# An LSTM recurrence on one core: smaller rooms for filler sums at the start, fewer sums in empty steps, and the first half of the late cells handed over in two pieces of 32 columns

## The chip, the cores and the metric

The kernel runs on one core of one Trainium2 chip. The metric is the device time of one execution in microseconds (us); the kernel before takes 3074.94 us, the median of three runs (3074.21 to 3075.44). All data are fp32.

## The reference, cut to what matters

The reference is an LSTM over 512 steps with a residual. Batch is 32, the input width 512, the hidden width 512.

```
xW = einsum('ntd,dg->ntg', x, Wx) + b        # x: 32 x 512 x 512, Wx: 512 x 2048
c = zeros_like(h0)
for each step t:
    a = xW[:, t] + h @ Wh                    # Wh: 512 x 2048
    i, f, o = sigmoid(a[:, :512]), sigmoid(a[:, 512:1024]), sigmoid(a[:, 1024:1536])
    g = tanh(a[:, 1536:])
    c = f * c + i * g
    h = o * tanh(c)
    out[:, t] = x[:, t] + h
```

## The kernel before, in words

**Steps.** The main loop goes over the 512 steps, `k`. A step has two parts on TensorE (PE). First comes the recurrent product `h @ Wh` of this step into the `gates` banks: 64 matmul instructions, in `h_part` (L1018) up to step 471 and in `h_halves` (L1032) from step 472 on, the "half steps". Then come products for the `x @ Wx` of later steps (L693, in the last steps also L935). While PE does these, the cell of the step is worked out: ScalarE (ACT) makes sigmoids and tanh (L1055 to L1057), VectorE (DVE) makes `fc`, `ig` and `c` (L1058 to L1060), ACT the tanh of `c` (L1061), DVE the product with the output gate (L1062) and its transposition into `ht` (L1063). The next recurrent product needs `ht`. So each step has two chains side by side, PE's filling products and the cell, and the longer one sets when the next recurrent product begins.

**x @ Wx.** These products are made for whole blocks of 32 steps (a "run") by a fast bilinear scheme: sums of input blocks ("nodes", L624; four small sums `s` per product, L652 to L655), products with sums of weight blocks, and sums of the products (L753, L763, L893, and L909 for the late ones, on DVE). Two short schemes for pairs of rows come first, and the weight sums are made once by DVE in the first steps (L452) and kept in memory (`keep_a`, `keep_b`). The program counts in window numbers `v = k + 16`; the runs begin at `v = START = 39` and take 32 steps each. Below, "rest n" is the n-th step of such a run. In the numbers n of a run's products there are gaps: some steps begin no product.

**The filler on DVE.** All DVE work that is not bound to the cell goes through a list. `push(window, columns, fn, ready)` enters a sum with the window number by which it has to be done; `run_due(v, room)` takes from the list what is due, and also what is not yet due as long as the room (in columns, 160 more for each sum) is not used up. The main loop calls it with `HEAD_ROOM` (5000) in the first steps, `ROOM` (4300) later and `HALF_ROOM` (2000) in the half steps. `evacuate`, which empties the PSUM banks of finished products, calls it once more, ahead of `third_sum` (`pp<-acc,p`, L763), with `BETWEEN` (1300) or, when no product was begun two windows before, twice that. What `run_due` takes in a step stands on DVE ahead of that step's `fc` (L1058), because the engine works in the order of the program.

**Half steps.** `cell_halves` works on 64 of 128 columns at a time. `gates_of(m)` has ACT make the gate functions of half `m` (L1077 to L1079), `sums_of(m)` has DVE make `fc`, `ig` and `c` (L1083 to L1085), ACT makes the tanh (L1098 and L1111), and `end_of(m)` has DVE multiply (L1089) and transpose (L1093). `h_halves` begins with `ht` of the columns of half 0, `k` = 0 and 1 (blocks of 32 columns of `ht`), into both halves of the gates, then takes `k` = 2 and 3. So PE's next step begins when the first half is transposed, and the second half has until the middle of the recurrent product.

**Ends.** The last sums of the last run go out in the first half steps; beside and after them come six late products (`describe_late`, with `t_sums`, weight sums on DVE at L405 to L407 into `nodes` and reloaded weights `raw_again`) and direct products (L935).

Of the kernel before, what the change touches and what calls it, by code (L numbers as in the profile page):

```python
# [15 lines left out]
B = 32  # L16
# [29 lines left out]
PER = ROW * MO  # L46
# [10 lines left out]
FIRST_SUMS = 1200  # L57
BETWEEN = 1300
HEAD_ROOM = 5000
FILL_ROOM = 3000  # L60
HALF_ROOM = 2000
SPACING = 5

LATE_ORDER = (1, 0, 2, 3, (0, (0, 1)), (0, (2, 3)))
# [252 lines left out]
def kernel(  # L317
# [400 lines left out]
    def evacuate(v, room):  # L718
        taken = run_due(v - 0.5, FIRST_SUMS if room else 0)
        taken += finish_halves(v)  # L720
        job = jobs.get(v - 1)
        if job and job.w >= EARLY:
            copy_first(job)
        for job in (jobs.get(v - 1), jobs.get(v - 2)):
            if job and job.w5 == v - 1 and job.w >= EARLY:
                copy_fifth(job)
        taken += second_sum(v)
        if v - 3 in jobs:
            taken += run_due(v, min(room - taken, BETWEEN if v - 2 in jobs else 2 * BETWEEN))
        return taken + third_sum(v)  # L730

    def evacuate_at_first(v):
# [140 lines left out]
    def finish_product(job, sb, n):  # L873
        c = sb.scheme

        def finish(half):
            pp = job.pp[half].rearrange("p n c -> p (n c)")
            if n in c.copied:
                if half == 0:
                    slot(sb, n)  # L880
                nc.scalar.copy(sums[sb, n][:, half], pp)

            def source(v):
                return pp if v == n else sums[sb, v][:, half]

            taken = 0

            for v in c.by_ready[n]:
                _, a, b = c.c_ops[v - c.r]
                if v in c.at_half:  # L890
                    if half == 0:
                        slot(sb, v)
                    add(c, v)(sums[sb, v][:, half], source(a), source(b))  # L893
                    taken += 4 * P + FIXED
                    if half == 1:
                        for u in (a, b):
                            if u != n or n in c.copied:
                                used(sb, u)
            if half == 0:
                return taken  # L900
            for v in c.by_ready[n]:
                if v in c.at_half:
                    put_out(sb, v)
                    continue

                def go(v=v):
                    _, a, b = c.c_ops[v - c.r]
                    slot(sb, v)
                    add(c, v)(sums[sb, v], sums[sb, a], sums[sb, b])  # L909
                    used(sb, a)  # L910
                    used(sb, b)
                    put_out(sb, v)

                push(
                    sb.at + c.limit[v] - 0.5,
                    8 * P,
                    go,
                    lambda at, v=v: all((sb, u) in sums for u in c.c_ops[v - c.r][1:])
                    and (last_use(sb, v) or len(sb.pool) > (at < sb.at + c.limit[v] - 0.5)),
                )  # L920
            return taken

        return finish
# [143 lines left out]
    def cell_halves(t):  # L1067
        n, tt = divmod(t, ROW)
        s = work.tile([P, G, P], F32, name=f"s_{t}", tag="s")
        fc = work.tile([P, P], F32, name=f"fc_{t}", tag="fc")  # L1070
        c = work.tile([P, P], F32, name=f"c_{t}", tag="c", bufs=2)
        ht = work.tile([P, NJ, B], F32, name=f"ht_{t}", tag="ht", bufs=3) if t < T - 1 else None
        us = [slice(m * HP, (m + 1) * HP) for m in range(2)]

        def gates_of(m):
            g, u = bank_half(m), us[m]
            nc.scalar.activation(s[:, 0:2, u], g[:, 0:2], AF.Sigmoid)  # L1077
            nc.scalar.activation(s[:, 2, u], g[:, 2], AF.Tanh)
            nc.scalar.activation(s[:, 3, u], g[:, 3], AF.Sigmoid)  # L1079

        def sums_of(m):
            u = us[m]
            nc.vector.tensor_mul(fc[:, u], s[:, 1, u], state["c"][:, u])  # L1083
            nc.vector.tensor_mul(ig[:, u], s[:, 0, u], s[:, 2, u])
            nc.vector.tensor_add(c[:, u], fc[:, u], ig[:, u])  # L1085

        def end_of(m):
            u = us[m]
            nc.vector.tensor_mul(fc[:, u], s[:, 3, u], ig[:, u])  # L1089
            if t == T - 1:  # L1090
                nc.vector.tensor_add(ig[:, u], fc[:, u], state["x"][:, u])
            else:
                nc.vector.transpose(ht[:, 2 * m : 2 * m + 2].rearrange("p q b -> p (q b)"), fc[:, u])  # L1093

        gates_of(0)
        seed_half(t + 1, 0)
        sums_of(0)
        nc.scalar.activation(ig[:, us[0]], c[:, us[0]], AF.Tanh)  # L1098
        if t == T - 1:
            gates_of(1)  # L1100
            sums_of(1)
            nc.scalar.activation(ig[:, us[1]], c[:, us[1]], AF.Tanh)
            end_of(0)
            end_of(1)
            nc.sync.dma_start(out=out[n][:, tt * P : (tt + 1) * P], in_=ig)
            return
        end_of(0)
        gates_of(1)
        seed_half(t + 1, 1)
        sums_of(1)  # L1110
        nc.scalar.activation(ig[:, us[1]], c[:, us[1]], AF.Tanh)  # L1111
        end_of(1)
        state["c"], state["ht"] = c, ht
        put_step(t)
# [78 lines left out]
    def describe_late(job, j):  # L1193
        def make(i):
            def begin():
                if not late_pairs:
                    assert len(node_free) == NODES
                    node_free.clear()
                    late_pairs.extend(node_pairs)
                tt_[i] = late_pairs.pop(0).rearrange("p m t e b -> p (m t e b)").rearrange("p (n c) -> p n c", c=C)  # L1200
                ops.extend(t_sums(i))
                ops.pop(0)()

            ops = []
            late_made[i] = []
            for m, columns in enumerate((2 * C, C, C)):

                def go(m=m):
                    (begin if m == 0 else ops.pop(0))()
                    late_made[i].append(m)  # L1210

                push(
                    job.w - 2 + 0.75 * m,
                    columns,
                    go,
                    lambda v, m=m: v >= LAST + 4 and len(late_made[i]) == m,
                )

        if isinstance(j, tuple):
            describe_half(job, *j)  # L1220
            return
        for i in (j, NJ + j):
            if i not in RESIDENT:
                make(i)
        if job.w == LATE_AT[0]:

            def both():
                f = free.pop(0).rearrange("p k (g t b) -> p k g t b", g=4, t=4)
                for k in range(2):
                    head_sums[LATE_ROW, k], more = inner_sums(block(raw_block(LATE_ROW, k)), f[:, k])  # L1230
                    late_ops.extend(more)
                late_ops.pop(0)()

            for m in range(8):
                push(
                    job.w - 2 + m / 4,
                    P,
                    lambda m=m: both() if m == 0 else late_ops.pop(0)(),
                    lambda v, m=m: v >= job.w - 2 and (len(late_ops) == 8 - m or m == 0),
                )  # L1240
        job.factors = lambda s: [
            (left(block(raw_block(LATE_ROW, k)), s, head_sums[LATE_ROW, k]), raw_factor(NJ * k + j, s)) for k in range(2)
        ]
        job.finish = finish_late(job, LATE_ROW, j)
# [52 lines left out]
    with tc.manual_schedule():  # L1297
# [70 lines left out]
        for k in range(T):  # L1368
            if k % 2 == 0 and k + 2 < T:
                load_residual(k + 2)  # L1370
            (h_part if k < HALVES else h_halves)(k)
            v = k + OFF
            if v < START + 14:
                head(v)
            announce(v)
            for op in prepare(v):
                op()
            room = HEAD_ROOM if v < START - 4 else ROOM if k < HALVES - 1 else HALF_ROOM
            run_due(v, room - evacuate(v, room))
            products(v)  # L1380
            tail_products(v)
            if k + 3 < LATE_END:
                load_xw(k + 3)
            fetch(v)
            if k == T - 2:
                x_last()
            if k + 4 < LATE_END:
                fill_bias(k + 4)
            (cell if k < HALVES else cell_halves)(k)
            seed_first(k + 2)  # L1390
            seed_last(k + 1)
# [52 lines left out]
```

## Time and profile before

| | before |
|---|---|
| median of 3 runs | 3074.94 us |
| profiled execution, its own time | 3074.57 us |
| its span | 3072.8 us |
| granted TensorE clock in it | 1.000 |
| DVE, ACT, POOL busy | 75%, 65%, 27% |
| DMA | 716.21 MB, 233 GB/s mean |

The span is the time between the first and the last recorded instruction of the profiled execution; its own time is 1.77 us longer. Busy time is given per engine, and the granted clock is the one at which TensorE was allowed to run. The chain of waits lists, in order of time, the piece of work that the end of the program depended on: start, length, engine, operation and line, number of instructions. In the groups of instructions the columns are line, engine, operation, tiles (out<-in), shapes and count, then total busy time and the mean ns of one, then the idle time just before them and what ended it. In the timeline a row has the start, the length, the engine, line and operation, and in brackets the idle time before it with what ended it. "issue" is time that the profile puts down to no wait.

### The profile page before, as it was taken

What the parts mean: (1) busy time and instruction counts of PE and PEld (TensorE: products, weight loads), DVE (VectorE), ACT (ScalarE), POOL (GpSimd) and SP (SyncE); (2) the same over time, 40 slices, a digit from 0 to 9 for tenths busy, and PEclk for the clock granted to TensorE, in tenths of its full rate; (3) what the DMA queues carried; (4) which work ended last, traced back from release to release, by engine and by line L of the source; (5) the groups of instructions that cost most, each with busy time, mean ns of one, the idle gap of its engine ahead of it and who ended that gap; (6) DMA issues with size and microseconds to landing.
All of it is one profiled execution on the core that took longest, in us unless ns stands there. A gap on an engine that the chain in (4) does not pass through costs nothing.

```text
span 3072.8 us, 133850 instructions
## 1 busy us (share of the span) xinstructions
PE 3064.4 (100%) x56568; PEld 2064.6 (67%) x56568; DVE 2314.5 (75%) x6545; ACT 2002.6 (65%) x5774; POOL 830.3 (27%) x1041
## 2 busy tenths in 40 slices
PE   9999999999999999999999999999999999999999
PEld 5566886666666666666666667866666666666666
DVE  7888777777777777777777777777777777777754
ACT  4666666666666666666666666666666666666664
POOL 0323222222222222222222222222222222222331
PEclk9999999999999999999999999999999999999999
DMA  9999887988889888898888988889788898888753
GB/s 326 294 271 268 233 247 213 255 231 236 246 210 259 224 244 238 218 263 216 254 231 212 267 214 248 232 223 260 216 254 232 223 255 222 250 232 219 196 120 71
DMA packets 345192, 716.21 MB, mean 233 GB/s; under 512 B 45712, under 2 KB 112016, under 8 KB 344080
## 3 DMA queue, kind: packets, MB, share of 16 engines
q1 hardware_dynamic: 268768, 564.74, 55.8%
q0 software_dynamic: 75392, 142.38, 27.6%
q8 instruction: 445, 7.29, 0.9%
q14 instruction: 155, 1.27, 0.1%
q10 hardware_dynamic: 432, 0.53, 0.1%
HBM read 521.48 MB, written 185.99 MB: 230 GB/s over the span
## 4 chain that ended last, share of the span: by engine, by line
PE 99%; DVE 1%; ACT 0%; DMA 0%; issue 0%; SPq 0%; DVEq 0%; ACTq 0%
PE gates L1018 53%; PE acc L693 18%; PE pp L693 18%; PE p L693 6%; PE gates L1032 4%; PE acc L935 0%; PE pp L935 0%; DMA raw_sb<-in_L_cond_Wx_dram 0%; DVE tt_sb L909 0%; PE gates L693 0%; DVE c L1085 0%; DVE fc L1089 0%; DVE fc L1083 0%; DVE ht L1093 0%; DVE nodes L405 0%
## 5 line engine op out<-in xcount | busy, mean ns | idle before, releaser
L1018 PE MATMUL gates<-wh_sb,ht 128*32 128x384 f32 (+1 forms) x30144 | 1739.2, 379 | 0.1
L1018 PEld LDWEIGHTS gates<-wh_sb,ht 128*32 128x32 f32 x30144 | 1083.8, 110 | 653.6 <-issue 554.9
L1121 POOL TENSOR_TENSOR oc<-xr,ht 128x128 f32<-128x128 f32 x509 | 384.6, 756 | 2101.8 <-DVE ht L1063 1916.6
L980 POOL DMA_DIRECT2D xw<-xw x508 | 447.1, 880 | 92.6 <-DVE s L652 62.5
L1055 ACT ACTIVATE s<-gates 128x256 f32<-128x256 f32 x472 | 182.0, 386 | 346.2 <-PE gates L1018 335.9
L693 PE MATMUL pp<-wb,nodes 128*32 128x256 f32 x4000 | 335.1, 379 | 0.0
L976 ACT COPY xw<-bias_sb 128x512 f32<-128x512 f32 x508 | 320.9, 632 | 0.0
L1058 DVE TENSOR_TENSOR fc<-s,c 128x128 f32<-128x128 f32 x471 | 136.6, 290 | 190.4 <-ACT s L1055 186.0
L761 ACT COPY pp<-pu 128x512 f32<-128x512 f32 x404 | 243.0, 602 | 47.5 <-DVE raw_sb L893 18.4
L1062 DVE TENSOR_TENSOR fc<-s,ig 128x128 f32<-128x128 f32 x472 | 137.8, 292 | 177.3 <-ACT ig L1061 177.3
L1057 ACT ACTIVATE s<-gates 128x128 f32<-128x128 f32 x472 | 131.2, 278 | 147.1 <-PE gates L1018 147.0
L693 PE MATMUL pp<-wb,s 128*32 128x256 f32 x2704 | 226.9, 379 | 0.0
L693 PE MATMUL acc<-wb,s 128*32 128x256 f32 x2704 | 226.9, 379 | 0.0
L693 PE MATMUL p<-wa,s 128*32 128x256 f32 x2704 | 226.7, 379 | 0.0
L763 DVE TENSOR_TENSOR pp<-acc,p 128x256 f32<-128x256 f32 x406 | 172.9, 426 | 71.4 <-ACT pp L762 69.0
L693 PE MATMUL acc<-wa,s 128*32 128x256 f32 x2704 | 226.4, 379 | 0.0
L1003 ACT COPY gates<-xw 128x384 f32<-128x384 f32 x472 | 223.2, 473 | 2.4 <-DMA xw<-xw 2.3
L762 ACT COPY pp<-acc 128x256 f32<-128x256 f32 x406 | 146.4, 361 | 108.0 <-DVE tt_sb L893 40.0
L1061 ACT ACTIVATE ig<-c 128x128 f32<-128x128 f32 x472 | 146.2, 310 | 101.0 <-DVE c L1060 60.8
L753 DVE TENSOR_TENSOR pu<-acc,p 128x256 f32<-128x256 f32 x404 | 167.4, 414 | 43.9 <-ACT p L772 35.4
L1063 DVE STREAM_TRANSPOSE ht<-fc 128x128 f32<-128x128 f32 x472 | 146.9, 311 | 50.3 <-DVE fc L1062 1.4
L772 ACT COPY p<-p 128x256 f32<-128x256 f32 x406 | 154.1, 379 | 37.1 <-PE p L693 34.9
(269 smaller groups left out, 4629.7 us busy)
## 6 DMA issues: line engine op xcount, KB each, us to landing
wb<-keep_b SPq DMA_DIRECT2D x338, 512.0 KB, 6.3
xw<-xw POOLq DMA_DIRECT2D x508, 256.0 KB, 5.8
wa<-keep_a SPq DMA_DIRECT2D x338, 384.0 KB, 5.3
xw<-tt_sb SPq DMA_DIRECT2D x404, 128.0 KB, 3.7
xw<-raw_sb SPq DMA_DIRECT2D x404, 128.0 KB, 3.9
xr<-in_x_dram SPq DMA_DIRECT2D x256, 128.0 KB, 5.5
out_dram<-oc SPq DMA_DIRECT2D x255, 128.0 KB, 4.5
row<-in_x_dram SPq DMA_DIRECT2D x63, 512.0 KB, 8.3
```

Source lines behind the costliest of these rows:

```text
L693: nc.tensor.matmul(dst[t * B : (t + 1) * B], a[:, t % a.shape[1]], w[t // a.shape[1]] if isinstance(w, list) else w, start=(s in (1, 5) or ...
L753: nc.vector.tensor_add(job.pu[:, 1], job.acc, job.p5)
L761: nc.scalar.copy(job.pp[0], job.pu)
L763: nc.vector.tensor_add(job.pp[1][:, 1], job.acc, job.p5)
L772: nc.scalar.copy(job.p5, p5[:, job.w if job.w < EARLY else 0])
L976: nc.scalar.copy(xw[t], bias_sb)
L980: nc.gpsimd.dma_start(out=xw[t], in_=stored[i][a], accum_op=mybir.AluOpType.add)
L1003: nc.scalar.copy(gates[t % 2][:, 0:IFG], xw[t][:, 0:IFG])
L1018: nc.tensor.matmul(g[j * B : (j + 1) * B, cols], state["ht"][:, k, :], wh_sb[:, k, j, cols], start=False, stop=True, skip_group_check=True,)
L1055: nc.scalar.activation(s[:, 0:2], g[:, 0:2], AF.Sigmoid)
L1063: nc.vector.transpose(ht.rearrange("p q b -> p (q b)"), h)
L1121: (nc.gpsimd if t < T - 3 else nc.vector).tensor_add(state["oc"][:, tt % 2], xr[t][:, tt % 2], ht)
```

## The change

Six small edits.

- In the main loop, up to `v = 38`, the room of a step is made smaller by 400 for every group of products that the step lacks (`FEWER`).
- In `evacuate`, the doubled `BETWEEN` room applies only up to `v = START + PER = 71`.
- In `finish_product`, the sums of the last run that carry the latest limit are due one window later.
- In `cell_halves`, `end_of(0)` multiplies and transposes two pieces of 32 columns: product, product, transposition, transposition. `end_of(1)` is as before. The very last step (`t == T - 1`) is as before.
- In `describe_late`, the weight sums `t_sums` are due half a window later (`job.w - 1.5` for `job.w - 2`).
- `HALF_ROOM` is 1800, not 2000.

```diff
+FEWER = 400
-HALF_ROOM = 2000
+HALF_ROOM = 1800
...
-            taken += run_due(v, min(room - taken, BETWEEN if v - 2 in jobs else 2 * BETWEEN))
+            taken += run_due(v, min(room - taken, BETWEEN if v - 2 in jobs or v > START + PER else 2 * BETWEEN))
...
                 push(
-                    sb.at + c.limit[v] - 0.5,
+                    sb.at + c.limit[v] - 0.5 + (sb is RUNS[-1] and c.limit[v] == max(c.limit.values())),
...
         def end_of(m):
             u = us[m]
-            nc.vector.tensor_mul(fc[:, u], s[:, 3, u], ig[:, u])
             if t == T - 1:
+                nc.vector.tensor_mul(fc[:, u], s[:, 3, u], ig[:, u])
                 nc.vector.tensor_add(ig[:, u], fc[:, u], state["x"][:, u])
-            else:
-                nc.vector.transpose(ht[:, 2 * m : 2 * m + 2].rearrange("p q b -> p (q b)"), fc[:, u])
+                return
+            ks = ((2 * m, 2 * m + 1), (2 * m + 1, 2 * m + 2)) if m == 0 else ((2 * m, 2 * m + 2),)
+            for a, b in ks:
+                nc.vector.tensor_mul(fc[:, a * B : b * B], s[:, 3, a * B : b * B], ig[:, a * B : b * B])
+            for a, b in ks:
+                nc.vector.transpose(ht[:, a:b].rearrange("p q b -> p (q b)"), fc[:, a * B : b * B])
...
-                    job.w - 2 + 0.75 * m,
+                    job.w - 1.5 + 0.75 * m,
...
             room = HEAD_ROOM if v < START - 4 else ROOM if k < HALVES - 1 else HALF_ROOM
+            if v < START:
+                room -= FEWER * sum(len(ss) for late, ss in IN_STEPS if v - late not in jobs and (late, ss) != (1, (5,)))
             run_due(v, room - evacuate(v, room))
```

The changed file has 7 more lines, so that L1058 of before is L1059 after, L1083 is L1084, and the product and transposition of the half steps are L1096 and L1098 for L1089 and L1093. The order of instructions changes on DVE in steps 11 to 30, in a few steps of each run, and from step 472 on. On PE and ACT it stays, except for the waits. On the queues of POOL and SP some stores of weight sums (`keep_a`, `keep_b`) stand one or two rows later, and one store of `xw` three rows later.

**DVE, rest 12 of a run.** In the steady runs, step 227 is a rest 12. The rows on DVE from the last sum `raw_sb<-tt_sb` (L909) of that step on, before:

```order
3016 L909 TENSOR_TENSOR raw_sb_93<-tt_sb_94 128x1024
3017 L654 TENSOR_TENSOR s2_231_9_23493<-nodes_0_164 128x128
3018 L653 TENSOR_TENSOR s1_231_10_23495<-s0_231_10_23392,nodes_1_165 128x128
3019 L763 TENSOR_TENSOR pp_2_88<-acc_0_83,p5_240_23381 128x256
3020 L1058 TENSOR_TENSOR fc_227_23532<-s_227_23531,c_226_23427 128x128
3021 L1059 TENSOR_TENSOR ig_170<-s_227_23531 128x128
3022 L1060 TENSOR_TENSOR c_227_23533<-fc_227_23532,ig_170 128x128
3023 L1062 TENSOR_TENSOR fc_227_23532<-s_227_23531,ig_170 128x128
3024 L1063 STREAM_TRANSPOSE ht_227_23534<-fc_227_23532 128x128
3025 L652 TENSOR_TENSOR s0_231_11_23582<-nodes_2_166 128x128
3026 L624 TENSOR_TENSOR nodes_4_168<-row_32_22651,nodes_4_168 128x512
```

And after, in the same step:

```order
3016 L910 TENSOR_TENSOR raw_sb_93<-tt_sb_94 128x1024
3017 L764 TENSOR_TENSOR pp_2_88<-acc_0_83,p5_240_23381 128x256
3018 L1059 TENSOR_TENSOR fc_227_23528<-s_227_23527,c_226_23427 128x128
3019 L1060 TENSOR_TENSOR ig_170<-s_227_23527 128x128
3020 L1061 TENSOR_TENSOR c_227_23529<-fc_227_23528,ig_170 128x128
3021 L1063 TENSOR_TENSOR fc_227_23528<-s_227_23527,ig_170 128x128
3022 L1064 STREAM_TRANSPOSE ht_227_23530<-fc_227_23528 128x128
3023 L655 TENSOR_TENSOR s2_231_9_23578<-nodes_0_164 128x128
3024 L654 TENSOR_TENSOR s1_231_10_23580<-s0_231_10_23392,nodes_1_165 128x128
3025 L653 TENSOR_TENSOR s0_231_11_23582<-nodes_2_166 128x128
```

The two small sums went from ahead of `fc` to behind the transposition; the node sum that came after them (L624) went on to step 230, and the one of step 230 to the start of step 231.

**DVE, a half step.** The first half of the cell in step 477, before:

```order
6137 L1083 TENSOR_TENSOR fc_477_47792<-s_477_47791,c_476_47715 128x64
6138 L1084 TENSOR_TENSOR ig_170<-s_477_47791 128x64
6139 L1085 TENSOR_TENSOR c_477_47793<-fc_477_47792,ig_170 128x64
6140 L1089 TENSOR_TENSOR fc_477_47792<-s_477_47791,ig_170 128x64
6141 L1093 STREAM_TRANSPOSE ht_477_47794<-fc_477_47792 128x64
```

And after, where one row stands for each pair of pieces:

```order
6137 L1084 TENSOR_TENSOR fc_477_47802<-s_477_47801,c_476_47723 128x64
6138 L1085 TENSOR_TENSOR ig_170<-s_477_47801 128x64
6139 L1086 TENSOR_TENSOR c_477_47803<-fc_477_47802,ig_170 128x64
6140 L1096 TENSOR_TENSOR fc_477_47802<-s_477_47801,ig_170 128x32 x2
6141 L1098 STREAM_TRANSPOSE ht_477_47804<-fc_477_47802 128x32 x2
```

The half step has two DVE instructions more, and both products stand ahead of the first transposition.

**PE, what waits for it.** The recurrent product that uses this `ht`, before:

```order
6647 L1032 MATMUL gates_81<-wh_sb,ht_47794 32x256 [waits DVE_49,Activation_49]
6648 L1032 MATMUL gates_81<-wh_sb,ht_47794 32x256 x7
6649 L1032 MATMUL gates_82<-wh_sb,ht_47794 32x256 [waits Activation_49]
6650 L1032 MATMUL gates_82<-wh_sb,ht_47794 32x256 x7
6651 L1032 MATMUL gates_81<-wh_sb,ht_47794 32x256 [waits DVE_49]
```

And after:

```order
6657 L1033 MATMUL gates_81<-wh_sb,ht_47804 32x256 [waits DVE_49,Activation_49]
6658 L1033 MATMUL gates_81<-wh_sb,ht_47804 32x256 x3
6659 L1033 MATMUL gates_81<-wh_sb,ht_47804 32x256 [waits DVE_49]
6660 L1033 MATMUL gates_81<-wh_sb,ht_47804 32x256 x3
6661 L1033 MATMUL gates_82<-wh_sb,ht_47804 32x256 [waits Activation_49]
```

The first four matmuls wait for the first transposition alone, the next four for the second.

More of the change, by code (lines that the diff above doesn't have):

```diff
@@ L918, in finish @@
                     lambda at, v=v: all((sb, u) in sums for u in c.c_ops[v - c.r][1:])
-                    and (last_use(sb, v) or len(sb.pool) > (at < sb.at + c.limit[v] - 0.5)),
+                    and (last_use(sb, v) or len(sb.pool) > (at < sb.at + c.limit[v] - 0.5 + (sb is RUNS[-1] and c.limit[v] == max(c.limit.values())))),
                 )
```

## The prediction

> **What bounds the kernel now.** I read the page's first table, then the chain of waits, then the timeline around the places where the chain lingers.
>
> ```profile
> span 3072.8 us, 133850 instructions
> PE 3064.4 (100%) x56568; PEld 2064.6 (67%) x56568; DVE 2314.5 (75%) x6545; ACT 2002.6 (65%) x5774; POOL 830.3 (27%) x1041
> ```
>
> PE is busy for all but 8.4 us, and the change takes no matmul away. A matmul that waits for its `ht` is counted as busy, though, so PE's true stalls are in the lengths of the chain's pieces. A recurrent product that waits for nothing takes 3.45:
>
> ```profile
> 1436.11 3.45 PE gates L1018 x64
> ```
>
> Of the longest pieces of the chain, these are longer; the excess over 3.45 is a stall, since the 64 matmuls are the same:
>
> ```profile
> 151.08 3.65 PE gates L1018 x64
> 163.49 3.62 PE gates L1018 x64
> 169.37 3.66 PE gates L1018 x64
> 217.06 3.63 PE gates L1018 x64
> ...
> 489.66 3.63 PE gates L1018 x64
> 495.48 3.66 PE gates L1018 x64
> 673.54 3.54 PE gates L1018 x64
> ...
> 874.07 3.52 PE gates L1018 x64
> ...
> 2755.38 3.54 PE gates L1018 x64
> ...
> 2894.48 3.54 PE gates L1032 x64
> ...
> 3054.61 3.53 PE gates L1032 x64
> ```
>
> Four kinds of place, then: single steps in the first 220 us; the first full run with all its sums, near 490 us; one step per run with 0.09 (twelve such runs, the first at 673.54, the last at 2755.38) and another, two steps later, with 0.07; and nearly each half step, with 0.08 to 0.11. Everything the change can win lies in these; the rest is PE at work.
>
> **The first steps and the first full run.** Beside the four rows above, a product row is too long there, and PE waits 0.10 more ahead of step 14:
>
> ```profile
> 155.16 0.86 PE acc L693 x16
> ...
> 161.22 0.98 PE acc L693 x16
> ...
> 169.27 0.10 issue
> ```
>
> So the stalls are 0.20 + 0.17 + 0.21 + 0.18, and 0.12 and 0.10: 0.98 us. At each of these places the change takes one or more large sums (a node, or a weight sum at L452) or two to three small sums from ahead of `fc`. A node lasts about 0.66, so it removes more than the longest stall, 0.31. The sums go to later steps, the last to step 29. I count 0.95 as gone and 0.03 as coming back in step 29, where a node stands just ahead of `fc`. Near 490 us:
>
> ```profile
> 483.87 3.52 PE gates L1018 x64
> ...
> 487.82 1.41 PE acc L693 x24
> ...
> 493.29 1.29 PE acc L693 x24
> ```
>
> 0.07 + 0.12 + 0.18 + 0.21 = 0.58. Two small sums leave the first of these steps, a node the second, and one small sum the third. For the third I need the price of a small sum on DVE, which comes with the next place.
>
> **The steady runs.** Here is a step before the 0.09 stall, in which the order shows the two small sums leave (ACT's tanh first, then DVE):
>
> ```profile
> 1427.29 0.27 ACT L1056 ACTIVATE s<-gates 128x128 f32<-128x128 f32 x1
> ...
> 1427.52 0.28 DVE L654 TENSOR_TENSOR s<-nodes 128x128 f32<-128x128 f32 x1
> 1427.72 0.28 DVE L653 TENSOR_TENSOR s<-s,nodes 128x128 f32<-128x128 f32 x1
> ...
> 1428.25 0.28 DVE L1058 TENSOR_TENSOR fc<-s,c 128x128 f32<-128x128 f32 x1
> ```
>
> `fc` could begin soon after 1427.56 and begins at 1428.25, behind DVE's queue, 0.69 late; all but 0.09 of that is hidden under PE's products. A small sum costs 0.20 of the queue (1427.52 to 1427.72, each starting while the one before still lasts). Two gone make `fc` 0.40 earlier, and the 0.09 vanishes. In the second place one small sum fewer stands ahead (0.20 against 0.07): gone too. Twelve runs by 0.16 are 1.92. At 490 us the third step keeps 0.21 - 0.20 = 0.01, so 0.57 of 0.58 goes.
>
> What leaves must go somewhere: a node goes to steps 230 and 231. The latter has this row in it:
>
> ```profile
> 1450.89 0.29 DVE L1058 TENSOR_TENSOR fc<-s,c 128x128 f32<-128x128 f32 x1 [1.03 <-ACT s L1055]
> ```
>
> DVE stood idle 1.03 ahead of `fc`, and 0.66 fits under it. Without that cover the 0.09 would come back, as a rival below.
>
> **Half steps: long sums.** In two steps `fc` is late. With the ACT rows it waits for:
>
> ```profile
> 2887.32 0.28 ACT L1077 ACTIVATE s<-gates 128x128 f32<-128x128 f32 x1 [0.42 <-PE gates L1032]
> ...
> 2887.88 0.21 DVE L1083 TENSOR_TENSOR fc<-s,c 128x64 f32<-128x64 f32 x1
> ...
> 2926.26 0.28 ACT L1077 ACTIVATE s<-gates 128x128 f32<-128x128 f32 x1 [1.43 <-PE gates L1032]
> ...
> 2927.02 0.21 DVE L1083 TENSOR_TENSOR fc<-s,c 128x64 f32<-128x64 f32 x1
> ```
>
> The sigmoids end at 2887.60 and 2926.54, so `fc` is 0.28 and 0.48 late, less 0.03 that it takes anyway: 0.25 and 0.45. In the first a weight sum (`nodes<-raw_again`) leaves, in the second one of two long sums (L909): 0.70 goes. Those weight sums now crowd into step 484, where I put back 0.05.
>
> **Half steps: the two pieces.** The tightest place of all, one half step from the tanh's end on:
>
> ```profile
> 2903.32 0.22 DVE L1089 TENSOR_TENSOR fc<-s,ig 128x64 f32<-128x64 f32 x1 [0.32 <-ACT ig L1098]
> ...
> 2903.68 0.24 DVE L1093 STREAM_TRANSPOSE ht<-fc 128x64 f32<-128x64 f32 x1
> ...
> 2903.84 0.18 DVE L1083 TENSOR_TENSOR fc<-s,c 128x64 f32<-128x64 f32 x1
> 2903.95 0.21 DVE L1084 TENSOR_TENSOR ig<-s 128x64 f32<-128x64 f32 x1
> ...
> 2904.07 3.66 PE L1032 MATMUL gates<-wh_sb,ht 128*32 128x256 f32 x64
> ```
>
> Product 0.22, gap 0.14, transposition 0.24, 0.15 to PE. What 32 columns cost is in no row; the groups of 128 and 64 columns give it:
>
> ```profile
> L1062 DVE TENSOR_TENSOR fc<-s,ig 128x128 f32<-128x128 f32 x472 | 137.8, 292 | 177.3 <-ACT ig L1061 177.3
> L1063 DVE STREAM_TRANSPOSE ht<-fc 128x128 f32<-128x128 f32 x472 | 146.9, 311 | 50.3 <-DVE fc L1062 1.4
> L1093 DVE STREAM_TRANSPOSE ht<-fc 128x64 f32<-128x64 f32 x78 | 19.1, 245 | 5.8
> L1089 DVE TENSOR_TENSOR fc<-s,ig 128x64 f32<-128x64 f32 x80 | 18.0, 225 | 25.1 <-ACT ig L1111 12.6 <-ACT ig L1098 12.6
> ```
>
> 64 columns less are 67 ns less for the product and 66 for the transposition, so 32 less are 34 and 33: estimates of 191 and 212. If the first piece's transposition begins one gap after its own product, `ht`'s first block is ready 67 ns earlier. This sits on the path in the 37 half steps that stall, and in the last step, which has nothing to hide it: 38 x 0.067 = 2.55. As each stall is 0.08 to 0.11, the gain is not cut off. The four matmuls that need only the first block take 4/64 of 3.66 = 0.23. The second transposition can begin 0.16 after the first (2903.68 to 2903.84), so its block comes 0.16 later: covered. The second half of the cell starts about 0.13 later, and its block is wanted only after 32 of 64 matmuls, 1.8 us into the product: covered.
>
> Bounds for this term: at best all stalls of 0.08 to 0.11 go, about 3.6 us; at worst the new pieces wait for each other and it costs time (rivals). I take 2.55, nearest to the rows of the same two operations.
>
> **The sum.** 0.95 - 0.03 + 0.57 + 1.92 + 0.70 - 0.05 = 4.06 for the moved filler, 2.55 for the pieces: 6.61. The profiled execution takes 3074.57 (its span plus 1.77), so 3067.96 after; its time lies 0.37 below the median of the runs, so as a median 3068.3, 0.22% less than 3074.94. About 0.2%, 6.15 us, is what a measurement of this kernel can tell from no change: the forecast stands just beyond it.
>
> **The rivals.**
>
> *The second product holds up the first transposition.* It stands between them on DVE. If the queue lets nothing begin before the product ends, the first transposition starts at 191 + 191 = 382 ns and ends at 594; today it ends at 225 + 135 + 245 = 605 (the gap of 0.14 in ns). The pieces then win nothing: 4.06 in all, 3074.94 - 4.06 = 3070.9. Against it: at 2903.84 and 2903.95 two independent operations start 0.11 apart while the first lasts 0.18. The Trainium skill, "VectorE: DVE Perf Modes", section "The DRAIN you can't avoid", has this rule: the next operation does not start until the pipe is empty. The pair above (0.11 against 0.18) disagrees with the rule as it stands; by the rule the time would be the 3070.9 of this case, by the pair the 3068.3 of the sum. Chance of this case 0.2, since no row shows an independent operation between a product and its transposition.
>
> *The moved sums make new late steps.* If the node of steps 230 and 231 or the small sums of rest 13 collide with PE's turn, the 0.09 comes back in twelve runs, 1.1 us; with 0.3 more in steps 13 to 29 the time is 3068.3 + 1.4 = 3069.7. For it: DVE is 75% busy and the list only moves work. Against it: the idle 1.03. Chance 0.17.
>
> *Slower.* Each of the four small operations waits for the end of the one before plus the gap of 135. Then products run at 0 and 326, the first transposition from 652 to 864 and the second from 999 to 1211: 259 later than today's 605 for the first, and the second block comes 347 after the first, 117 past the 0.23 of cover. 38 x 0.376 = 14.3 lost against 4.06 won: 3074.94 + 10.2 = 3085.2. It decides from 4.06 / 38 = 0.107 per half step on. For it: this is how `fc` and `ht` stand today, one after the other. Against it: those two depend on each other, and the first transposition does not depend on the second product. Chance 0.04.
>
> **How the numbers follow.** The forecast's case has 0.59. Its own range is 3066.9 to 3069.6: the pieces between 1.3 (half of it) and 3.6, and 0.3 for the runs' spread. The range that holds 8 in 10 reaches on to the first rival and ends at 3071.2; it leaves out the slow rival and the tails. Faster by over 0.2% means under 3068.8: some 0.47 from the forecast's case, whose middle is 0.5 inside that limit, and 0.03 from the second rival. The first rival, most of the second and the rest of the forecast's case are within 0.2%.
>
> **What would show it.** Right: the recurrent products at the places listed take 3.45 in the chain, the half steps 3.47 to 3.50; DVE's first transposition of 32 columns starts about 0.33 after its product starts, and PE 0.15 after its end. The first rival: that transposition starts no earlier than the second product's end. The second: pieces of 3.5 and more at rest 13 to 16 or in steps 15 to 30. The slow one: half steps of 3.8 and more, and PE waiting at its fifth matmul. The forecast is wrong if the chain loses those stalls and the time does not follow, or if the pieces win under 1 us.

## The result, and the profile after

The changed kernel takes 3069.55 us, the median of 17 runs (3068.01 to 3072.28), the kernel before 3074.43 us (3073.88 to 3075.44, 17 runs): 4.88 us less, a ratio of 0.9984 with a 95% interval of 0.9977 to 0.9990. The profiled execution of the changed kernel took 3069.55 us, its span is 3067.8, and the granted clock 1.000. The forecast was 3068.3: right in its sign, 1.25 too low, and with 0.16% the gain lies just inside the 0.2% that the prediction called no change. The gain itself is 1.73 short of the 6.61 that were summed: the median of three runs from which the forecast started stands 0.51 above the one of 17 runs here, and that hides part of the miss.

The first table of the page, of after:

```profile
span 3067.8 us, 133930 instructions
PE 3058.4 (100%) x56568; PEld 2011.7 (66%) x56568; DVE 2322.0 (76%) x6623; ACT 2001.9 (65%) x5774; POOL 834.1 (27%) x1041
...
PE 96%; DVE 1%; DMA 1%; issue 1%; ACT 0%; POOL 0%; SPq 0%; DVEq 0%; POOLq 0%; ACTq 0%
```

PE has as many matmuls as before and 6.0 us less of busy time, since a matmul that waits counts as busy; DVE has its 78 instructions more (6623 for 6545). New in the last line are DMA and POOL: the chain no longer runs along PE everywhere. Its longest pieces:

```profile
172.09 9.74 DMA xw<-xw
201.93 9.43 DMA xw<-xw
259.85 3.66 PE gates L1019 x64
...
295.45 3.54 PE gates L1019 x64
...
2882.65 3.47 PE gates L1033 x64
...
2896.93 3.50 PE gates L1033 x64
...
2935.14 3.60 PE gates L1033 x64
...
3049.82 3.47 PE gates L1033 x64
```

The four long products of the first 220 us, those near 490 us and those of 3.54 and 3.52 in the steady runs are gone; one of 3.54 stays, from rest 12 of the run ahead of window 72, to which the new rule does not apply (and one of 3.52 two steps later). The half steps take 3.46 to 3.50 for 3.53 to 3.56; the one of 3.60 is step 485. New are two loads of `xw` of over 9 us, in the first 220 us, and the 3.66 of step 30.

Where the time went, step by step: the start of each recurrent product after, less its start before, and by how much this difference moves.

| place | moved by, us | forecast, us |
|---|---|---|
| steps 12, 14, 15 | -0.17, -0.28, -0.31 | -0.77 |
| steps 18, 23, 30 | +0.30, +0.61, +0.89 | -0.18 at 23, +0.03 behind it |
| steps 68 to 70 (first full run) | -0.74 | -0.57 |
| rest 13 and 15 (the steps after 12 and 14) in twelve runs | -1.87 | -1.92 |
| steps 475 and 483, beyond the pieces | -0.24, -0.43 | -0.25, -0.45 |
| step 485, beyond the pieces | +0.14 | +0.05 |
| 38 half steps, 0.066 each | -2.52 | -2.55 |

In the profiled execution of before there were 0.39 more at steps 296 and 324 that no other trace of this study has. With them, 0.05 at step 42 and 0.04 in many small places the sum is -4.9, from step 0 to step 511.

### The profile page after: what moved, and what is told of

It reads as the page before. It is cut to its first block, busy times and chain, and to the rows that moved or that the text cites. A ratio compares the mean times of both kernels' runs of the same rounds, so it can differ in the third digit from the quotient of the medians.

```text
span 3067.8 us, 133930 instructions
## 1 busy us (share of the span) xinstructions
PE 3058.4 (100%) x56568; PEld 2011.7 (66%) x56568; DVE 2322.0 (76%) x6623; ACT 2001.9 (65%) x5774; POOL 834.1 (27%) x1041
## 4 chain that ended last, share of the span: by engine, by line
PE 96%; DVE 1%; DMA 1%; issue 1%; ACT 0%; POOL 0%; SPq 0%; DVEq 0%; POOLq 0%; ACTq 0%
PE gates L1019 51%; PE acc L694 17%; PE pp L694 17%; PE p L694 6%; PE gates L1033 4%; DMA xw<-xw 1%; DVE scratch L453 0%; PE acc L936 0%; PE pp L936 0%; DMA raw_sb<-in_L_cond_Wx_dram 0%; POOL oc L1126 0%; DVE raw_sb L894 0%; DMA xw<-nodes 0%; DMA xw<-raw_sb 0%; PE gates L694 0%
## 5 line engine op out<-in xcount | busy, mean ns | idle before, releaser
L1019 PEld LDWEIGHTS gates<-wh_sb,ht 128*32 128x32 f32 x30144 | 1041.1, 110 | 688.2 <-issue 609.6
L694 PE MATMUL pp<-wb,nodes 128*32 128x256 f32 x4000 | 320.4, 379 | 0.0
L1059 DVE TENSOR_TENSOR fc<-s,c 128x128 f32<-128x128 f32 x471 | 136.7, 290 | 169.1 <-ACT s L1056 165.6
L1058 ACT ACTIVATE s<-gates 128x128 f32<-128x128 f32 x472 | 131.3, 278 | 146.0 <-PE gates L1019 146.0
L694 PE MATMUL pp<-wb,s 128*32 128x256 f32 x2704 | 216.6, 379 | 0.0
L694 PE MATMUL acc<-wb,s 128*32 128x256 f32 x2704 | 216.6, 379 | 0.0
L694 PE MATMUL p<-wa,s 128*32 128x256 f32 x2704 | 216.5, 379 | 0.0
L694 PE MATMUL acc<-wa,s 128*32 128x256 f32 x2704 | 216.5, 379 | 0.0
```

The lines of the kernel that those rows point to most:

```text
L694: nc.tensor.matmul(dst[t * B : (t + 1) * B], a[:, t % a.shape[1]], w[t // a.shape[1]] if isinstance(w, list) else w, start=(s in (1, 5) or ...
L1019: nc.tensor.matmul(g[j * B : (j + 1) * B, cols], state["ht"][:, k, :], wh_sb[:, k, j, cols], start=False, stop=True, skip_group_check=True,)
```

## The experiments

**The theory and its rival.** Every term but one came out within 0.2 of the forecast. The one is the head: steps 18, 23 and 30. Here is GpSimd's queue (POOL in the rows) in the first of them, before and then after:

```profile
169.31 0.81 POOL L1121 TENSOR_TENSOR oc<-xr,ht 128x128 f32<-128x128 f32 x1 [3.48 <-DVE ht L1063]
170.07 0.87 POOL L980 DMA_DIRECT2D xw<-xw  x1
```

```profile
168.14 0.60 POOL L1126 TENSOR_TENSOR oc<-xr,ht 128x128 f32<-128x128 f32 x1 [4.42 <-DVE ht L1064]
171.39 0.61 POOL L485 DMA_DIRECT2D keep_a<-scratch  x1 [2.64 <-DVE scratch L453]
172.09 0.85 POOL L981 DMA_DIRECT2D xw<-xw  x1
...
181.91 0.48 ACT L1004 COPY gates<-xw 128x384 f32<-128x384 f32 x1 [2.63 <-DMA xw<-xw]
```

After, a store of a finished weight sum (`keep_a`, 384 KB) stands ahead of the load of `xw`. It waits 2.64 for its sum on DVE (L453), which `FEWER` has moved. So the load starts 3.35 after the end of the addition `oc`, not right behind it, and it shares its queue with the store. ACT, which fills the gates from `xw`, waits 2.63 for it. (Ahead of step 23 ACT waits 2.36 in the same way, ahead of steps 29 and 30 1.20 and 1.09.) *Theory A (stores ahead of loads):* this makes the 1.80 of the head. *Theory B (traffic):* the loads were slow by themselves, in this execution, whatever the order. A would also account for the spread of the runs, 4.3 us after and 1.6 before: 0.3 to 0.9 at a time, depending on when a transfer lands. The spread does not decide, though: e5 below, without `FEWER`, and e8, with loads ahead of stores, each have a run 4.5 us above the median.

**e1, without FEWER.**

```diff
-FEWER = 400
+FEWER = 0
```

> The changed kernel with FEWER = 0, so that the rooms of the first 38 windows are those of before. Theory A (stores ahead of loads): with FEWER the weight sums (L453) end later, their stores wait at the head of GpSimd's queue, the load of xw behind them starts late, and the cell or the sums wait for it: 0.30 + 0.61 + 0.89 = 1.80 us lost at steps 18, 23 and 30 of the profile, against 0.76 won at steps 12 to 15. Without FEWER both go: 3069.55 + 0.76 - 1.80 = 3068.5, and the runs spread by 1.5 us as those of before do, not by 4. Theory B (traffic): the loads of xw were slow by themselves, whatever the order: 3069.55 + 0.76 = 3070.3, and the spread stays at 4.

Measured: 3068.98 (3068.55 to 3073.77, 11 runs; 3074.47 for before), ratio 0.9984 (0.9975 to 0.9993). Nine of 11 runs lie within 1 us, the other two at 3073.5 and 3073.8, so the spread is 5.2 and not the 1.5 that A expected. By the median the kernel is no slower without its first edit; the interval, 0.0018 or 5.5 us wide, holds the 3068.5 of A and the 3070.3 of B. The trace speaks for A: the head has the stalls of before (0.18 of them at step 23) and none of the late steps 18, 23 and 30. The total that ACT waits for `xw`, in the waits (us, times, longest) of before, after and e1:

```profile
ACT gates L1003 <- DMA xw<-xw: 2.3, 5, 0.8
```

```profile
ACT gates L1004 <- DMA xw<-xw: 8.1, 6, 2.6
```

```profile
ACT gates L1004 <- DMA xw<-xw: 0.7, 2, 0.4
```

**e2, FEWER alone, on the kernel before.**

```diff
+FEWER = 400
...
+            if v < START:
+                room -= FEWER * sum(len(ss) for late, ss in IN_STEPS if v - late not in jobs and (late, ss) != (1, (5,)))
```

> The kernel before with FEWER alone. Theory A: 3074.43 - 0.76 + 1.80 = 3075.5, a spread of 3 us or more, and stalls near steps 18, 23 and 30. Theory B: 3074.43 - 0.76 = 3073.7, with the spread of before.

Measured: 3075.84 (3073.94 to 3076.76), ratio 1.0004 (0.9995 to 1.0013). The edit by itself wins nothing. The interval holds both theories; the trace agrees with A:

```profile
173.24 9.83 DMA xw<-xw
188.19 3.66 PE gates L1019 x64
218.91 3.66 PE gates L1019 x64
...
255.10 3.66 PE gates L1019 x64
```

In another execution steps 18, 23 and 29 are late by 0.39, 1.20 and 0.36 against before, where in the changed kernel it was 18, 23 and 30, and the long load is at the same place. Chance alone would hardly pick them twice. (Another 1.08 of this execution comes ahead of step 1, behind a load `xw<-nodes`, and concerns neither theory.)

**e3, the pieces alone, on the kernel before.**

```diff
         def end_of(m):
...
+            ks = ((2 * m, 2 * m + 1), (2 * m + 1, 2 * m + 2)) if m == 0 else ((2 * m, 2 * m + 2),)
+            for a, b in ks:
+                nc.vector.tensor_mul(fc[:, a * B : b * B], s[:, 3, a * B : b * B], ig[:, a * B : b * B])
+            for a, b in ks:
+                nc.vector.transpose(ht[:, a:b].rearrange("p q b -> p (q b)"), fc[:, a * B : b * B])
```

> The kernel before with the two pieces of 32 columns in the half steps alone. The sum of the prediction: 38 x 0.067 = 2.55 won, 3071.9, and the half steps' recurrent products at 3.46 to 3.50 for 3.53 to 3.56. Rival (the second product holds up the first transposition): no gain, 3074.4.

Measured: 3073.02 (3071.94 to 3074.80), ratio 0.9996 (0.9987 to 1.0005): 1.45 less, short of 2.55 by 1.1. The interval holds the forecast and the rival; the trace has the gain. Step by step, 0.06 to 0.07 is won in each half step, but 0.23 is lost at step 482 and 0.04 at 483. (Steps 38 and 68 are 0.22 and 0.17 later than in before; why was not tried.) The chain ahead of step 482:

```profile
2917.55 0.21 DVE ht L1097
2917.76 0.17 issue
2917.93 0.21 DVE ht L1097
...
2920.50 0.95 DVE nodes L405
2921.45 0.13 DVE fc L1083
```

The second transposition starts 0.38 after the first (0.14 in the other steps), the second half of the cell and DVE's sums behind it move back by as much, and this is a step in which two long sums stand ahead of `fc`. Such a hitch has a fixed place. Number all records of DVE in a trace from 0, in order of time and with the semaphore events: this transposition is number 7359, which leaves 63 when divided by 128. In the twelve traces 64 transpositions of 128 x 128 start 0.75 after their product and not 0.40: they are the 64 whose number leaves 63, and no others. No run shows why. In the changed kernel number 7359 is a semaphore event, and no step is late there. The profile's 2.0 in the half steps and the 1.45 of the medians differ by less than the interval.

**e4, loads ahead of stores, on the changed kernel.** The store of a weight sum is put on GpSimd's queue after the step's load of `xw`:

```diff
-                (nc.sync if at < OFF else nc.gpsimd).dma_start(out=kept[n][k // 2], in_=t[k // 2].rearrange("p n c -> p (n c)"))
+                go = lambda q: q.dma_start(out=kept[n][k // 2], in_=t[k // 2].rearrange("p n c -> p (n c)"))
+                if at < OFF:
+                    go(nc.sync)
+                else:
+                    held.append((n, k // 2, lambda: go(nc.gpsimd)))
+                    return
...
             if k + 3 < LATE_END:
                 load_xw(k + 3)
+            for n, part_of, keep_it in held:
+                keep_it()
+                stored_sums.add((n, part_of))
+            held.clear()
```

> The changed kernel, but from step 0 on the stores of finished weight sums stand behind the load of xw of their step on GpSimd's queue, not ahead of it. Nothing else moves. Theory A: the 1.80 us at steps 18, 23 and 30 go, the 0.76 stays: 3069.55 - 1.80 = 3067.8, and the spread falls below 2 us. Theory B: no difference, 3069.6.

Measured: 3068.11 (3067.58 to 3070.38; ten of 11 runs below 3068.71), ratio 0.9980 (0.9971 to 0.9989). A expected 3067.8. One run makes the spread 2.8, where A expected under 2. The queue at the same place:

```profile
168.09 0.60 POOL L1131 TENSOR_TENSOR oc<-xr,ht 128x128 f32<-128x128 f32 x1 [3.88 <-DMA xr<-in_x_dram]
168.75 0.90 POOL L986 DMA_DIRECT2D xw<-xw  x1
171.33 0.58 POOL L485 DMA_DIRECT2D keep_a<-scratch  x1 [1.68 <-DVE scratch L453]
```

The store still waits for its sum, but the load has gone right behind `oc` (0.06 after its end, for 3.35), and ACT's wait for `xw` is in no row of the waits any more. Of all kernels here this is the fastest by the median, 1.4 below the change itself. Against the fastest trace of each step, five of its steps are late by over 0.06: 0.09 and 0.07 at rest 12 and 14 of the early run, 0.08 ahead of step 474, 0.14 in step 484, and 0.28 ahead of step 42. The last is no load, as the expectation of e8 has it, but a late transposition on DVE, number 831 of its records:

```profile
327.41 0.29 DVE L1068 TENSOR_TENSOR fc<-s,ig 128x128 f32<-128x128 f32 x1 [0.38 <-ACT ig L1067]
328.16 0.31 DVE L1069 STREAM_TRANSPOSE ht<-fc 128x128 f32<-128x128 f32 x1 [0.46 <-DVE fc L1068]
```

**e5, the rule on BETWEEN alone, on the kernel before.**

```diff
-            taken += run_due(v, min(room - taken, BETWEEN if v - 2 in jobs else 2 * BETWEEN))
+            taken += run_due(v, min(room - taken, BETWEEN if v - 2 in jobs or v > START + PER else 2 * BETWEEN))
```

> The kernel before with the rule on BETWEEN alone (no doubled room from window 72 on). The sum of the prediction: 0.57 at the first full run and 1.92 in the twelve later ones, 2.49 won: 3074.47 - 2.49 = 3072.0, every recurrent product at rest 12 and 14 at 3.45, and the two small sums behind the transposition. Rival (the sums make new late steps where they land): 0.09 back in twelve steps, 3073.1.

Measured: 3072.33 (3071.48 to 3076.84; before 3074.62), ratio 0.9993 (0.9984 to 1.0002): 2.3 less, as the sum had it. Of the stalls of over 0.06 none is left between 306 us and the half steps. The trace also has one of 0.74 ahead of step 31, where ACT waited up to 1.8 for `xw`: a slow load can strike without `FEWER` too, so B keeps a part.

**e6, product and transposition in turn, on e4.**

```diff
             for a, b in ks:
                 nc.vector.tensor_mul(fc[:, a * B : b * B], s[:, 3, a * B : b * B], ig[:, a * B : b * B])
-            for a, b in ks:
                 nc.vector.transpose(ht[:, a:b].rearrange("p q b -> p (q b)"), fc[:, a * B : b * B])
```

> The kernel of e4 (3068.11), with the four small operations of the half step as product, transposition, product, transposition. Theory (each transposition waits for its own product and then 0.135 us): the first transposition starts 0.33 after its product as now, the second product starts only behind it, and the second block comes some 0.1 too late for PE's fifth matmul: 36 x 0.09 = 3.2 lost, 3071.3. Rival (the second product holds up the first transposition): that one starts up to 0.1 earlier, the rest of the stalls, 0.01 to 0.05, goes: 36 x 0.03 = 1.1 won, 3067.0.

Measured: 3068.82 (3068.22 to 3070.50), ratio 0.9982 (0.9973 to 0.9991). Neither. In the timeline of one half step:

```profile
2899.00 0.19 DVE L1101 TENSOR_TENSOR fc<-s,ig 128x32 f32<-128x32 f32 x1 [0.32 <-ACT ig L1107]
...
2899.32 0.21 DVE L1102 STREAM_TRANSPOSE ht<-fc 128x32 f32<-128x32 f32 x1
2899.46 0.15 DVE L1101 TENSOR_TENSOR fc<-s,ig 128x32 f32<-128x32 f32 x1
2899.64 0.21 DVE L1102 STREAM_TRANSPOSE ht<-fc 128x32 f32<-128x32 f32 x1
2899.68 0.85 PE L1038 MATMUL gates<-wh_sb,ht 128*32 128x256 f32 x12
```

The first transposition starts 0.32 after its product with nothing between them, as it does with the second product between them: that product holds nothing up, and the rival falls. My own price falls too: the second block is 0.32 behind the first, and PE's first twelve matmuls run through in 0.85, the length that they had in before. Each group of four matmuls starts 0.215 after the one before, so the fifth starts at 2899.89, 0.04 after the end of the second transposition. From the end of the first transposition that is 0.36, since PE's 0.15 ahead of its first matmul counts as cover too. (The weight loads of the first eight matmuls have all begun by 2899.73 on record, before the block is finished, so the rows don't show when PE read it.) Per half step e6 and e4 are equal. What e6 lost, 1.1 in its trace, sits in three steps (481, 485 and 503) in which DVE is late. The first is the hitch of e3, at number 7359 again; the other two have other numbers and stay open:

```profile
2913.96 0.21 DVE L1102 STREAM_TRANSPOSE ht<-fc 128x32 f32<-128x32 f32 x1 [0.46 <-DVE fc L1101]
```

**e7, the first half whole, on e4.**

```diff
+            nc.vector.tensor_mul(fc[:, u], s[:, 3, u], ig[:, u])
             if t == T - 1:
-                nc.vector.tensor_mul(fc[:, u], s[:, 3, u], ig[:, u])
                 nc.vector.tensor_add(ig[:, u], fc[:, u], state["x"][:, u])
-                return
...
+            else:
+                nc.vector.transpose(ht[:, 2 * m : 2 * m + 2].rearrange("p q b -> p (q b)"), fc[:, u])
```

> The kernel of e4 without the pieces: product and transposition of the first half whole, as before. If the pieces are worth 38 x 0.067 = 2.55 where nothing else is late in the half steps: 3068.11 + 2.55 = 3070.7. If they are worth only the 1.45 that they brought alone: 3069.6.

Measured: 3070.79 (3070.24 to 3073.06), ratio 0.9988 (0.9979 to 0.9997): by the medians the pieces are worth 2.68 on e4, where the late sums have been moved out of their way. In the traces 2.2 of it lie in the half steps, 0.062 in each of 35; 0.36 more is a hitch at step 491 (number 7487) that e4 does not have, so the close agreement with 2.55 is in part luck. The half steps are back at 3.53 to 3.56:

```profile
2895.91 3.56 PE gates L1038 x64
...
2905.62 3.53 PE gates L1038 x64
```

**e8, the last two stalls of e4.**

```diff
-HALF_ROOM = 1800
+HALF_ROOM = 1700
...
-            taken += run_due(v, min(room - taken, BETWEEN if v - 2 in jobs or v > START + PER else 2 * BETWEEN))
+            taken += run_due(v, min(room - taken, BETWEEN if v - 2 in jobs or v > START else 2 * BETWEEN))
```

> The kernel of e4 with HALF_ROOM = 1700, so that one weight sum less stands in step 484, and with the undoubled BETWEEN in the run ahead of the first full one too. e4 has three stalls left between step 0 and the last: 0.30 at a load in the first steps, 0.09 at rest 12 of that run, 0.15 in step 484. Two of them go: 3068.11 - 0.22 = 3067.9, and their places show 3.45 and 3.47 in the chain. Rival (the sum moved on from step 484 makes the next step late): 3068.1.

Measured: 3068.77 (3067.62 to 3073.35), ratio 0.9982 (0.9973 to 0.9991). No gain. Both stalls are gone from the trace, but there are two new ones. About 1 us comes ahead of step 1, behind a load, as in e2:

```profile
67.54 4.38 DMA xw<-nodes
```

The other, 0.44 ahead of step 31, is the price of the second edit. With the smaller room in step 30 two node sums (L630) that stood ahead of `pp` in e4 stand behind it. DVE waits for ACT ahead of `pp`, and then three node sums hold up `fc`:

```profile
261.07 0.43 DVE L769 TENSOR_TENSOR pp<-acc,p 128x256 f32<-128x256 f32 x1 [0.67 <-ACT pp L768]
261.41 0.68 DVE L630 TENSOR_TENSOR nodes<-row,row 128x512 f32<-128x512 f32 x1
262.12 1.29 DVE L630 TENSOR_TENSOR nodes<-nodes,row 128x512 f32<-128x512 f32 x2
263.34 0.28 DVE L1064 TENSOR_TENSOR fc<-s,c 128x128 f32<-128x128 f32 x1
```

So the edit loses more (0.44) than the stalls that it removes (0.09, 0.07 and 0.14): a moved sum did make a new late step, though not the one that the rival named.

**e9 and e10, on the kernel before: FEWER with loads ahead of stores, and that order alone.** The edits are those of e2 and e4 together, and of e4.

> The kernel before with FEWER, and with the stores of weight sums behind the load of xw of their step, as in e4. FEWER without that gave 3075.84 (e2). Theory A (stores ahead of loads): FEWER wins its 0.95 here: 3074.5 - 0.95 = 3073.5, and the three late steps of e2 (18, 23 and 29) are gone. Theory B (traffic): as e2, 3075.5 or more.

> The kernel before with nothing but the stores of weight sums behind the load of xw of their step. Theory A: in the kernel before, the sums end early enough that their stores hold up no load, so the time stays at 3074.5, within 0.5. Theory B': the order on the queue is worth something whatever FEWER does, and e4's gain over the changed kernel (1.44) is mostly that: 3073.0.

Measured: e9 3074.13 (3073.35 to 3074.59), ratio 0.9998 (0.9989 to 1.0007); e10 3074.47 (3074.10 to 3076.59), ratio 1.0001 (0.9993 to 1.0010), with 3074.49 for before. e10 is A's answer: in the kernel before no store holds up a load at a price, and the order is worth nothing. e9 is 1.7 below e2, and its trace has none of the three late steps, nor those of before: every recurrent product from 145 to 229 us takes

```profile
168.51 3.45 PE gates L1024 x64
174.56 3.45 PE gates L1024 x64
```

So the order of store and load is what `FEWER` needs. Whether it helps by the earlier start of the load or by a landing without the store beside it, these runs don't separate. `FEWER`'s own gain came out smaller than 0.95: 0.34 from e10 to e9, and 0.87 from e1 to e4. The traces of e9 and e2 name part of the rest: 0.6 less at steps 68 to 70 than in before, but 0.15 more at each of two steps near 1820 us, for which no cause was looked for, and 0.18 and 0.35 at steps 483 and 491, where DVE's numbers 7359 and 7487 are `ig` and the transposition. How much of that the medians hold, with runs that spread by 1.2, stays open.

## Why the prediction was right, and where not

**What bounds the kernel.** Right: all that was won lay in the recurrent products longer than 3.45, and the sum over the places gives the measured time (-4.9 in the trace, -4.88 in the medians). That the two agree is in part luck, as the trace of before has 0.39 of hitches that others lack.

**The pieces.** Right to 0.03 us of 2.55. The estimates of 191 and 212 ns were met: the group of first and second products has a mean of 189, and the transposition one of 191, the first of each pair taking 211.

```profile
L1098 DVE STREAM_TRANSPOSE ht<-fc 128x32 f32<-128x32 f32 x78 | 12.0, 191 | 1.0 <-DVE fc L1096 0.4 <-DVE ht L1098 0.2
L1096 DVE TENSOR_TENSOR fc<-s,ig 128x32 f32<-128x32 f32 x78 | 11.5, 189 | 12.6 <-ACT ig L1103 12.6
```

The first transposition starts 0.33 after its product, and PE 0.15 after its end, as the prediction asked. The rival of the second product fell in e6, the slow one with it. One part of the reasoning was wrong and cost nothing: the cover of the second block is 0.36, counted from the end of the first transposition, and not 0.23 (e6).

**The steady runs and the first full run.** Right: 1.87 for 1.92, 0.74 for 0.57, and e5 alone 2.3 for 2.49. The node that goes to steps 230 and 231 was covered, so the rival of new late steps fell here. At rest 12 after, DVE's `pp` and `fc`:

```profile
1427.19 0.43 DVE L764 TENSOR_TENSOR pp<-acc,p 128x256 f32<-128x256 f32 x1
1427.53 0.28 DVE L1059 TENSOR_TENSOR fc<-s,c 128x128 f32<-128x128 f32 x1
```

0.34 apart, with no small sums ahead, and the recurrent product at 1430.09 takes 3.45. The 0.74 cannot be put down to this edit alone: in e9, without it, most of that excess is gone too.

**The long sums of the half steps.** Right for the two that go (0.67 for 0.70); step 484 got 0.14 for 0.05, as three weight sums stand ahead of `pp` and `fc` there, one of them longer (0.57) than its like elsewhere (0.38):

```profile
2931.38 0.65 DVE L406 TENSOR_TENSOR nodes<-tt_sb 128x512 f32<-128x512 f32 x1
2932.07 0.57 DVE L407 TENSOR_TENSOR nodes<-tt_sb,nodes 128x256 f32<-128x256 f32 x1
2932.56 0.68 DVE L406 TENSOR_TENSOR nodes<-raw_again 128x512 f32<-128x512 f32 x1
2933.16 0.42 DVE L764 TENSOR_TENSOR pp<-acc,p 128x256 f32<-128x256 f32 x1
```

**The first steps: the step that failed.** "I count 0.95 as gone and 0.03 as coming back in step 29" was right in its first half: the stalls on DVE went. But the sums that were moved are inputs of stores, and I followed them on DVE alone. Their stores stand ahead of the loads of `xw` on GpSimd's queue, where the order of rows shows them one place later. That cost 1.80 in the profile (e4 and e9 take it away, e10 shows that the order is free where the sums are early), and turned the term from -0.92 to -0.76 + 1.80 = +1.04. It is the rival of moved sums that make new late steps, with the place wrong: not the 0.09 of rest 13 to 16, nor 0.3 in the head, but a queue on another engine. That the time is near this rival's 3069.7 is chance, as its twelve stalls did not come back. The 1.96 are more than the 1.73 by which the gain fell short; some 0.3 of small misses stand beside them, and on the other side 0.17 more than summed at the first full run and the 0.39 of hitches in the profiled execution of before.

**The range.** The forecast's own case was to end at 3069.6 (with the terms that it names, 1.3 for the pieces and 0.3 for the spread, it is 3068.3 + 1.25 + 0.3 = 3069.9). That 3069.55 lies inside is luck: the term of the first steps was wrong by 1.96, and the start of the sum was 0.51 too high. From 3074.43 the same sum would have forecast 3067.8.

## What to carry to other kernels

When work is moved to a later place on one engine, follow what it feeds as well: a store that waits for it holds up every later entry of its queue, and the loss appears some steps on, at whoever uses the load behind it. Put loads with a due time ahead of stores that have none. A stall of 0.1 us that recurs is safely priced from the rows of the two chains that race; a place where a transfer decides varies more from run to run than such a stall is worth.

## What the runs showed of the hardware

- An independent DVE operation of 128 x 32 starts 0.11 us after the one before it, which lasts 0.19; a transposition that depends on that one starts 0.33 after it, with or without another operation between them.
- From the end of the transposition to PE's first matmul pass 0.15 us when PE stands still. In e6 the matmul that needs the second block starts 0.04 after the recorded end of that block's transposition, in a stream of other matmuls.
- The load of `xw` (256 KB) that stands right behind the store of 384 KB took 9.7 and 9.8 us to land in after and e2. At the same place it took 8.2 in before, with no store ahead, and 7.2 and 5.7 in e4 and e9, with the store behind it. Other loads right behind a store took 4.3 to 10.4 us, so the store is not all that counts; the median of all these loads is 5.8 in before.
- A transposition on DVE is 0.35 late where its number among DVE's records leaves 63 when divided by 128: all 64 such transpositions of 128 x 128 in the twelve traces, and none of that shape elsewhere. The sum `c` at such numbers is never late (71 of 71), and no row says why. Traces with the same order on DVE have the hitch at the same operations, so an edit that adds or moves instructions also moves it on or off the critical path. Other single delays, 0.22 and 0.56 at steps 485 and 503 of e6, are not at such numbers.
